# A two-layer perceiver block: the keys' constant, the norms' powers and the values' bias computed elsewhere, and a new order

## The chip, the cores and the metric

The kernel runs on one core of one Trainium2 chip. A core has TensorE (PE, matrix products into PSUM), VectorE (DVE), ScalarE (ACT), GpSimd (POOL) and SyncE (SP), which here starts all transfers. Each engine runs its own instructions in order; engines wait for each other on semaphores. The metric is the device time of one execution in microseconds (us), lower is better; a kernel's time is the median of its runs.

## The reference

The input `x` has 128 batches of 32 tokens, 256 wide; the context `ctx` has 128 batches of 257 rows, 256 wide. Six residual steps follow each other:

```
x = x + xattn0(ctx, layernorm(x))        # softmax attention of x over the 257 context rows
x = x + scan(layernorm(x))               # gated selective scan, 512 channels x 16 states, 32 steps
x = x + mlp0(layernorm(x))               # ternary weights, gelu, layernorm inside, hidden 1024
x = x + xattn1(layernorm(x), ctx, ctx)   # focused linear attention over the context, 16 heads
x = x + attn1(layernorm(x))              # attention among the 32 tokens, low-rank keys and values
x = x + mlp1(layernorm(x))               # quantized activations (127 steps), ternary weights
```

The change sits mostly in `xattn1`, cut here to what matters:

```
def feature(x, scale):
    x = (relu(x) + 1e-6) / scale
    xp = x ** 3
    return xp / norm(xp) * norm(x)
q = feature(input_q @ Wq + bq, sp)
k = feature(input_k @ Wk + bk, sp)
v = input_v @ Wv + bv
z = 1 / (einsum(q, k.sum(axis=2)) + 1e-6)
kv = einsum('bhjc,bhjd->bhcd', k, v)
out = einsum('bhic,bhcd->bhid', q, kv) * z
```

## The kernel before

**Tiling.** Four batches make a group: 4 x 32 = 128 tokens, one row of a tile each. There are 32 groups, taken in nine blocks of 2, 4, 4, 4, 4, 4, 4, 4 and 2 groups (`BLOCKS`). For each group, `context_group` loads its context, computes `xattn0` and then sums `k` times `v` over the 257 keys for `xattn1` (result `kvc`; the last context row is treated apart, through `pl`, `vl`, `plg`, `vlz`). For each block, `scan_block` does the scan for all its tokens at once (up to 512 columns). For each group, `latent_group` then runs `mlp`, `linear` (the query side of `xattn1`), `attention` and `quantized_mlp`, and stores the group.

**Order.** Nothing runs where it is written. Every call on `R` is recorded, with the engines that could do it (`R.either` is DVE or POOL; `relu`, `copy`, `cast`, `scaled` and `minus_column` also offer two), its duration as estimated by `ns_of`, and the operations it needs. `Recorder.order` then places all operations in a list schedule: each part of the work has a span of due times in `DUE`, an operation's due time lies inside its part's span, and of the operations that can start within `WINDOW` of the first, the one with the earliest wanted time is taken. Where an operation has several engines, `chosen` takes the one with the smallest sum of start and duration times (1 + `PRICE` of the engine). `trace` emits the result and chains the instructions of each engine in exactly that order; its line L575 issues every recorded instruction, which is why the trace shows that line nearly everywhere. Where the plan leaves TensorE idle for more than 600 ns, `keep_busy` (L562) adds matmuls of constants. Buffers come from rings of fixed size.

**Keys and values.** For two batches at a time, `keys` forms the keys `z` in PSUM (tile `pkey`): a matmul of ones with `bk3` brings in the scaled bias, three bf16 parts that add up to it, then come the products with `wkv[:, 0]`. `bk3` is built during setup from `bk` by way of `parts`: four row groups of 32 with the same content, of which batch i of the pair uses rows 32 i to 32 i + 2. `keys_values` then makes `u = relu(z)` (ACT, tile `ku`), adds the constant `e1` = 1e-6/scale on POOL, and calls `cubed`. That takes sums of squares on ACT (tile `ks`, with sums in `kn`), multiplies on POOL to get the cube, takes sums of squares again, raises the two sums to the powers 1/2 and -1/2 in one POOL operation with the tile `halves`, and multiplies the two into the factor `f` (tile `kf`). The values (`pval`) are scaled by `f` on ACT into `vf`, whose seventeenth column per head is `f` itself, and `pk` collects the sums over keys. For the queries, `cubed` runs once per group with the inverse factor (tiles `ls`, `ln`, `lf`).

**Norms.** `stats` takes mean and variance on DVE (`st`, `mv`) and `rstd_of` forms (variance + eps) to the power -1/2 in two POOL operations (`rstd`). `norm` then writes `xn = (x - mean) * rstd` on DVE. In `scan_block` this runs for each group, followed by the addition of `b_out` on POOL, transposes into `xTs`, the projections `pproj` and, per state, `a` (ACT), the scan `h` (DVE) and the weighted sum `acc` (DVE) or `some` (POOL).

**Bias of the values.** `linear` multiplies `bv1` by the denominators `den` on POOL (tile `y`), adds the numerators from PSUM (`pn`) on DVE and multiplies by `zf` on DVE.

**Quantizing.** `quantize` forms 127/max as a reciprocal and a multiplication on DVE (`qm`), multiplies and rounds in two operations: for the 256-wide input on DVE and then POOL, for the 1024-wide one on POOL (DVE in the last block).

Of the kernel before, what the change touches and what calls it, by code (L numbers as in the profile page):

```python
# [16 lines left out]
P = 128  # L17
# [249 lines left out]
class Recorder:  # L267
# [62 lines left out]
    def record(self, calls):  # L330
        ways = {}
        for engine, (name, args, kw) in calls.items():
            out = kw.get("out", args[0] if args else None)
            rest = list(args[1:] if "out" not in kw else args)
            rest += [v for k, v in kw.items() if k not in ("out", "accum_out")]
            ins = [a for a in rest if is_ap(a)]
            outs = [a for a in (out, kw.get("accum_out")) if is_ap(a)]
            full = dict(kw)
            if name == "tensor_scalar":
                full |= dict(zip(("scalar1", "scalar2"), args[2:4]))  # L340
            if name == "scalar_tensor_tensor":
                full |= dict(zip(("scalar",), args[2:3]))
            if name == "activation":
                full |= dict(zip(("func",), args[2:3]))
            if engine == "gpsimd" and name == "tensor_tensor":
                full |= dict(zip(("op",), args[3:4]))
            n = size_of(out)
            ns = ns_of(engine, name, full, out, ins, n)
            table = TABLES.get(full.get("func")) if name == "activation" else None
            tensors = [  # L350
                a for a in ins if (size_of(a) > 1 or name == "tensor_tensor") and not in_psum(a)
            ]
            locks = engine == "gpsimd" and len(ins) > 0
            if engine == "vector":
                two = name in ("tensor_tensor", "scalar_tensor_tensor", "tensor_tensor_scan")
                fast = name in ("tensor_scalar", "tensor_copy") and not in_psum(out)
                locks = len(tensors) > 1 if two else fast and len(tensors) > 0 and n > 64
            ways[engine] = [(name, args, kw)], ns, locks
        reads = [b for b in map(box_of, ins) if b]
        writes = [b for b in map(box_of, outs) if b]  # L360
        bufs = [a.buf for a in (*ins, *outs) if isinstance(a, View)]
        self.keep += bufs
        self.bufs_of.update((id(b), b) for b in bufs)
        if self.joined is not None:
            small = ins[0].shape[0] < P or size_of(ins[0]) < P
            self.joined.append((*ways["tensor"][:2], reads, writes, small))
            return
        landing = 0
        if "sync" in ways:
            size = size_of(out) * P * 4 if writes else 0  # L370
            landing = 2000 + size / 180.0
        self.add(ways, reads, writes, table, landing)
# [218 lines left out]
PRICE = {"tensor": 0.0, "vector": 28.013093, "scalar": 4.356996, "gpsimd": 3.720234, "sync": 0.0}  # L591
WINDOW = 13.821085
SOONER = 0.0675
AHEAD = 0.744939
HORIZON = 1.665209
# [3 lines left out]
def perceiver_kernel(ctx: ExitStack, tc: tile.TileContext, t: dict, out: bass.AP):  # L599
# [30 lines left out]
    nc.gpsimd.memset(halves[:, 1, :], 0.5)  # L630
    ones = cst.tile([P, P], F32, name="ones")
# [96 lines left out]
    bv1 = row("bv1", t["bv1"], D)  # L728
# [36 lines left out]
    def cubed(u, n, tag, inverse=False):  # L765

        sq = (t2k if n == 2 else t1k)([P, n, D], f"{tag}s")
        nrm = tiny(f"{tag}n", [P, 2, n])
        for j in range(n):
            R.scalar.activation(sq[:, j, :], u[:, j, :], AF.Square, accum_out=nrm[:, 0, j : j + 1])  # L770
        R.gpsimd.tensor_tensor(u, sq, u, ALU.mult)
        for j in range(n):
            R.scalar.activation(sq[:, j, :], u[:, j, :], AF.Square, accum_out=nrm[:, 1, j : j + 1])
        powers = halves[:, 0:2, 0:n] if inverse else halves[:, 1:3, 0:n]
        R.gpsimd.tensor_tensor(nrm, nrm, powers, ALU.pow)
        f = tiny(f"{tag}f", [P, n])
        R.gpsimd.tensor_tensor(f, nrm[:, 0, :], nrm[:, 1, :], ALU.mult)
        return f
# [58 lines left out]
    R.vector.tensor_tensor(bk, bk, col, ALU.mult)  # L837

    parts = t1k([P, 2, 4, 32], "bkp")
    R.gpsimd.memset(parts, 0.0)  # L840
    for k in range(3):
        part = ring("bkb", 1).tile([P, 2], "bkb", BF16)
        R.vector.tensor_copy(part, bk)
        R.vector.tensor_copy(parts[:, :, :, k], part.unsqueeze(2).to_broadcast([P, 2, 4]))
        if k < 2:
            R.vector.tensor_tensor(bk, bk, parts[:, :, 0, k], ALU.subtract)
# [24 lines left out]
    R.vector.tensor_scalar(p_l[:, 0, :], pkl[:, 0:D], 0.0, None, ALU.max)  # L871
    R.vector.tensor_tensor(p_l[:, 0, :], p_l[:, 0, :], e1, ALU.add)
# [88 lines left out]
    def stats(xg):  # L961

        st = tiny("st", [P, 6])
        R.vector.bn_stats(st, xg)
        mv = tiny("mv", [P, 2])
        R.vector.bn_aggr(mv, st)
        return mv, rstd_of(mv[:, 1:2], LN_EPS)

    def norm(xg):
        mv, r = stats(xg)  # L970
        xn = t1k([P, D], "xn")
        R.vector.tensor_scalar(xn, xg, mv[:, 0:1], r, ALU.subtract, ALU.mult)
        return xn, mv, r
# [19 lines left out]
    def context_group(b0, xg, kvc):  # L993
# [91 lines left out]
        with R.together():  # L1085
            for m in range(8):
# [6 lines left out]
                )  # L1093
        for b in range(0, GB, PAIR):
            zs = keys(cTs[b : b + PAIR])
            for i in range(PAIR):
                keys_values(cTs[b + i], zs[i], pk[:, :, b + i, :], b + i == GB - 1)
        v = pk.rearrange("p c b (h k) -> p h c b k", h=2)
        R.vector.tensor_scalar(kvc, v[:, 0], odd[:, 0:1], None, ALU.mult)
        R.vector.scalar_tensor_tensor(kvc, v[:, 1], odd[:, 1:2], kvc, ALU.mult, ALU.add)  # L1100

# [19 lines left out]
    def keys_values(cT, z, pk, last):  # L1121
        u = t2k([P, 2, D], "ku")
        R.relu(u, z)
        R.gpsimd.tensor_tensor(u, u, e1.unsqueeze(1).to_broadcast([P, 2, D]), ALU.add)
        f = cubed(u, 2, "k")
        R.first = (len(R.ops) - 3,)
# [10 lines left out]
        for j in range(2):  # L1137
            R.scalar.activation(
                vf[:, j, :, 0:16], pv[:, j * D : (j + 1) * D].rearrange("p (h k) -> p h k", k=16),
                AF.Copy, scale=f[:, j : j + 1],  # L1140
            )
        R.gpsimd.tensor_copy(vf[:, :, :, 16], f.unsqueeze(2).to_broadcast([P, 2, NH]))
        with R.together():
            for c in range(2):
                for j in range(2):
                    for m in range(4 * c, 4 * c + 4):
# [5 lines left out]
                        )  # L1152


    def scan_block(x, late):
# [3 lines left out]
        xT = ring("xTs", 1).tile([P, 2, TOK], "xTs")[:, :, 0:tok]  # L1159
        for g in range(size):  # L1160
            xn, _, _ = norm(x[g])
# [97 lines left out]
    def linear(xg, kvc):  # L1259
# [23 lines left out]
        with R.together():  # L1283
# [8 lines left out]
        den = tiny("den", [P, NH], 2)  # L1292
        R.vector.tensor_copy(den, pv[:, :, 16])
# [7 lines left out]
        R.gpsimd.tensor_tensor(  # L1301
            yv, bv1.rearrange("p (h k) -> p h k", k=16),
            den.unsqueeze(2).to_broadcast([P, NH, 16]), ALU.mult,
        )
        R.vector.tensor_tensor(yv, pv[:, :, 0:16], yv, ALU.add)
        R.vector.tensor_tensor(yv, yv, zf.unsqueeze(2).to_broadcast([P, NH, 16]), ALU.mult)
# [102 lines left out]
    def quantize(h, n, ms, k, amax, gamma, late):  # L1409
# [10 lines left out]
        R.vector.tensor_scalar(m, m, 127.0, None, ALU.mult)  # L1420
# [4 lines left out]
        engine = wide if n == HID else R.vector  # L1425
        engine.tensor_scalar(h, h, m, ROUND, ALU.mult, ALU.add)
        q = (t2k if n == HID else t1k)([P, n], f"q{n}", BF16)
        engine = wide if n == HID else R.gpsimd
# [84 lines left out]
    (-1.233024, -0.335498), (0.019828, 0.480193), (-1.629912, -0.869437), (-0.837897, -0.738361),  # L1513
    (-0.093681, -0.088914), (-0.021839, -0.017211), (0.306149, 0.488484), (0.39917, 0.543159),
    (0.505346, 1.339487), (0.48714, 0.600075), (0.577018, 0.904067), (0.865508, 1.005891),
    (1.046044, 1.425814), (1.390255, 1.643429), (1.317874, 1.43935), (1.798509, 1.951231),
    (2.102721, 2.277249), (2.253363, 2.602763), (2.83034, 2.835295), (1.877067, 1.881711),
    (1.451009, 1.899495), (0.786758, 1.881711), (1.887508, 2.002024), (0.636118, 0.718999),
    (0.728345, 0.76535), (0.753626, 0.774222), (0.721695, 1.041519), (1.02934, 1.176199),
    (1.193086, 1.242338), (1.482066, 1.506436), (1.570038, 1.574756), (1.52572, 1.568128),  # L1520
    (1.582666, 1.870871), (1.996577, 2.069774), (2.143081, 2.422113), (2.358304, 2.65149),
    (2.69793, 2.755759), (2.394754, 2.76594), (2.909432, 3.128141), (3.227729, 3.512565),
    (3.409932, 3.76627), (2.727973, 3.098836), (3.085723, 3.337484), (3.365331, 3.681179),
    (3.656735, 4.119898), (2.875393, 3.198347), (3.111345, 3.33781), (3.418247, 3.706203),
    (3.705912, 4.06225), (3.050509, 3.381501), (3.357332, 3.56083), (3.584301, 3.855628),
    (3.839172, 4.228837), (1.635373, 1.790687), (1.595887, 1.641535), (1.962785, 2.117782),
    (2.053357, 2.161526), (2.195383, 2.199528), (2.205476, 2.209605), (2.389908, 2.395792),
    (2.486901, 2.49243), (2.488439, 2.647508), (2.615044, 2.87897), (2.840922, 3.128108),
# [125 lines left out]
```

## Time and profile before

| what | value |
|---|---|
| three runs | 1712.74, 1715.9, 1718.06 us |
| median | 1715.9 us |
| first to last instruction of the profiled execution | 1714.2 us (its own device time is not given apart) |
| mean granted TensorE clock | 0.996 |
| idle time of DVE, ACT, POOL between instructions | 209.5, 286.8, 345.3 us |
| share of the 16 DMA engines, 0 to 100 us | 0.52 |
| the same, 1000 to 1100 us | 0.11 |

The busy time of an engine is the time covered by its instructions. The chain of waits follows the last instruction back to what released it, step by step; its shares tell which engine the end was waiting for. PE's busy time contains the tails of pipelined matmuls: matmuls 256 wide in fp32 start 216 ns apart in a row, while a single one is shown with some 385 ns. In groups by shape, "128x4 f32<-128x4 f32" is the output and input (partitions x elements) of one instruction.

### The profile page before, as it was taken

The page shows a single profiled execution, that of the slowest core. Times are in us where ns is not written, and L with a number is a line of the kernel's source. Part 1 is how long each engine was busy: PE and PEld are TensorE (multiplying, and loading weights), DVE is VectorE, ACT ScalarE, POOL GpSimd, SP SyncE. Part 2 cuts the span into 40 slices and gives each one's busy share as a digit, 9 for nine tenths or more (in the row PEclk, how much of TensorE's full clock was granted, in tenths as well). Part 3 has the DMA queues.
Part 4 walks back from the last instruction along what each step waited for, and adds up shares of the span by engine and source line. Part 5 has one row for each costly group of instructions (what it writes and reads, how often), then busy time and mean ns, then how long its engine had stood idle before and what let it go on. Part 6 is the DMA issues. An engine that isn't in the chain of part 4 may idle for free.

```text
span 1714.2 us, 45797 instructions
## 1 busy us (share of the span) xinstructions
PE 1650.3 (96%) x17587; PEld 1200.9 (70%) x17587; DVE 1501.8 (88%) x2960; ACT 1422.8 (83%) x3484; POOL 1362.6 (79%) x2152
## 2 busy tenths in 40 slices
PE   8999999999999999999999999999999989899986
PEld 6778777767677767766777777777777666666664
DVE  5389699988997997959998997979999899999777
ACT  4587789888988899779888998889998888788676
POOL 6668769768795888688878678886898699788887
PEclk9999999999999999999999999999999999999999
DMA  8312100110010102001100012010110000000000
GB/s 235 99 60 72 30 29 30 57 35 7 29 54 5 35 14 63 30 2 45 38 30 29 8 42 63 3 29 10 61 42 30 2 20 8 4 4 2 5 9 22
DMA packets 44762, 59.74 MB, mean 35 GB/s; under 512 B 8704, under 2 KB 27008, under 8 KB 44544
## 3 DMA queue, kind: packets, MB, share of 16 engines
q1 hardware_dynamic: 44544, 56.81, 10.7%
q8 instruction: 139, 2.28, 0.6%
q14 instruction: 79, 0.65, 0.1%
HBM read 52.32 MB, written 4.19 MB: 33 GB/s over the span
## 4 chain that ended last, share of the span: by engine, by line
PE 48%; DVE 24%; ACT 15%; POOL 10%; issue 3%; DMA 0%; DVEq 0%; POOLq 0%; ACTq 0%; SPq 0%
DVE h L575 10%; PE pkey L575 7%; PE pproj L575 7%; PE pval L575 6%; DVE acc L575 5%; PE pT L575 3%; PE pmlp L575 3%; PE pqa L575 3%; POOL ku L575 3%; ACT a L575 2%; PE pk L575 2%; ACT ks L575 2%; ACT L575 2%; PE pka L575 2%; PE pcT L575 2%
## 5 line engine op out<-in xcount | busy, mean ns | idle before, releaser
L575 DVE TENSOR_TENSOR_SCAN h<-a,pproj 128x512 f32<-128x512 f32 (+1 forms) x576 | 613.9, 1087 | 22.6 <-ACT a L575 12.5
L575 ACT ACTIVATE a<-dl,a_neg 128x496 f32<-128x496 f32 (+1 forms) x576 | 367.5, 664 | 57.7 <-DVE h L575 53.6
L575 DVE SCALAR_TENSOR_TENSOR acc<-h,w_st,acc 128x512 f32<-128x512 f32 (+1 forms) x436 | 299.9, 688 | 0.7
L575 PE MATMUL pval<-wkv,cT 128*128 128x256 f32 x1024 | 243.9, 384 | 0.1
L575 PE MATMUL pkey<-wkv,cT 128*128 128x256 f32 x1024 | 238.1, 386 | 0.0
L575 ACT ACTIVATE ks<-ku 128x256 f32<-128x256 f32 x512 | 209.1, 415 | 19.3 <-POOL ku L575 17.9
L575 PEld LDWEIGHTS pkey<-wkv,cT 128*128 128x128 f32 x1024 | 189.3, 190 | 39.0 <-issue 15.6
L575 PEld LDWEIGHTS pval<-wkv,cT 128*128 128x128 f32 x1024 | 188.0, 190 | 32.0 <-issue 4.5
L575 POOL TENSOR_TENSOR ku<-ku,e 128x512 f32<-128x512 f32 x128 | 162.8, 1280 | 31.3 <-ACT ku L575 30.0
L575 POOL TENSOR_TENSOR ku<-ks,ku 128x512 f32<-128x512 f32 x128 | 164.4, 1290 | 16.9 <-ACT ks L575 15.8
L575 POOL TENSOR_TENSOR kn<-kn,halves 128x4 f32<-128x4 f32 x128 | 134.3, 1052 | 23.5 <-ACT ks L575 21.9
L575 ACT ACTIVATE vf<-pval,kf 128x256 f32<-128x256 f32 x256 | 108.3, 475 | 31.1 <-PE pval L575 26.3
L575 POOL TENSOR_TENSOR rstd<-rstd,halves 128x1 f32<-128x1 f32 x224 | 126.1, 567 | 6.1
L575 PE MATMUL pproj<-xTs,w_in 128*128 128x512 f32 (+1 forms) x288 | 122.8, 554 | 2.2 <-DVE x L575 1.3
L575 ACT ACT_TABLE_LOAD x95 | 121.9, 1283 | 2.3 <-DVE hq L575 0.6
L575 POOL TENSOR_TENSOR some<-some,h 128x512 f32<-128x512 f32 (+1 forms) x104 | 115.2, 1107 | 3.5
L575 PE MATMUL pmlp<-w_pr,hT 128*128 128x256 f32 x512 | 117.3, 383 | 0.6 <-DVE x L575 0.6
L575 PEld LDWEIGHTS pmlp<-w_pr,hT 128*128 128x128 f32 x512 | 96.2, 191 | 14.7 <-DVE x L575 0.7
L575 POOL TENSOR_SCALAR h<-h,w_st 128x512 f32<-128x512 f32 (+1 forms) x104 | 65.3, 629 | 51.0 <-DVE h L575 32.7
L575 ACT ACTIVATION_READ_ACCUMULATOR ks<-ku 128x1 f32 x512 | 100.8, 197 | 0.0
L575 POOL TENSOR_SCALAR rstd<-mv 128x1 f32<-128x1 f32 x224 | 45.4, 203 | 67.5 <-DVE mv L575 43.3
L575 PE MATMUL ph<-w_fc,x 128*128 128x512 bf16 x384 | 91.5, 380 | 0.3 <-ACT vf L575 0.2
(289 smaller groups left out, 3867.0 us busy)
## 6 DMA issues: line engine op xcount, KB each, us to landing
cx<-in_ctx_dram SPq DMA_DIRECT2D x64, 512.0 KB
x<-in_x_dram SPq DMA_DIRECT2D x32, 128.0 KB
cr<-in_ctx_dram SPq DMA_DIRECT2D x128, 32.0 KB
out_dram<-x SPq DMA_DIRECT2D x32, 128.0 KB
vlz<-vl SPq DMA_DIRECT2D x128, 1.1 KB
w_in<-in_w_inT_dram SPq DMA_DIRECT2D x1, 1024.0 KB
raw_fc<-in_w_fcT_dram SPq DMA_DIRECT2D x2, 512.0 KB
raw_pr<-in_w_prT_dram SPq DMA_DIRECT2D x2, 512.0 KB
```

What stands on the lines that cost most here:

```text
L575: ins = getattr(engine, name)(*(traced(a) for a in args), **{k: traced(v) for k, v in kw.items()}).ins
```

## The change

1. `bk3` is built from two columns, `bk + e1` and `bk`. The first batch of each pair reads the rows with the first one, so `u = max(z, e1)` in one DVE operation gives relu + e1. The second batch keeps relu on ACT and the addition on POOL. The row of `ctx` treated apart uses the first form too.
2. `cubed` takes the reciprocal of one sum of squares on DVE, multiplies by the other and raises the product to 1/2 in a single power half as wide. In `scan_block` the norms of all groups of a block share one power; its moments come first for all groups, then the power, then each group's `xn`.
3. `linear` no longer adds the values' bias: `context_group` adds bias times the sums of the keys to `kvc`, with two operations per group (tile `vb`). `bv1` comes as a column layout `bvc`, in 16 transfers in place of one.
4. `xn`, the multiplication by 127 and both steps of the narrow quantizing may run on DVE or POOL; the scaling of the values by `f` may be one DVE or two ACT operations. `record` takes lists of calls for that. The last batch of a group adds to `pk` after the other three.
5. `DUE` (every number, as many as before), `PRICE`, `WINDOW`, `SOONER`, `AHEAD` and `HORIZON` have new values.

```diff
-PRICE = {"tensor": 0.0, "vector": 28.013093, "scalar": 4.356996, "gpsimd": 3.720234, "sync": 0.0}
-WINDOW = 13.821085
-SOONER = 0.0675
-AHEAD = 0.744939
-HORIZON = 1.665209
+PRICE = {"tensor": 0.0, "vector": 903.348472, "scalar": 4.458506, "gpsimd": 4.513973, "sync": 0.0}
+WINDOW = 13.478919
+SOONER = 0.068234
+AHEAD = 0.632901
+HORIZON = 1.528864
...
-    bv1 = row("bv1", t["bv1"], D)
+    bvc = wts.tile([P, 2, 16], F32, name="bvc")
+    for c in range(2):
+        for h in range(8):
+            h_ = slice((c * 8 + h) * 16, (c * 8 + h + 1) * 16)
+            R.sync.dma_start(bvc[h * 16 : (h + 1) * 16, c, :], t["bv1"][:, h_].to_broadcast([16, 16]))
...
-        powers = halves[:, 0:2, 0:n] if inverse else halves[:, 1:3, 0:n]
-        R.gpsimd.tensor_tensor(nrm, nrm, powers, ALU.pow)
         f = tiny(f"{tag}f", [P, n])
-        R.gpsimd.tensor_tensor(f, nrm[:, 0, :], nrm[:, 1, :], ALU.mult)
+        R.vector.reciprocal(f, nrm[:, 1 - inverse, :])
+        R.either.tensor_tensor(f, f, nrm[:, inverse, :], ALU.mult)
+        R.gpsimd.tensor_tensor(f, f, halves[:, 1, 0:n], ALU.pow)
         return f
...
+    bks = tiny("bks", [P, 2, 2], 1)
+    R.vector.scalar_tensor_tensor(bks[:, :, 0], col, FOCUS_EPS, bk, ALU.mult, ALU.add)
+    R.vector.tensor_copy(bks[:, :, 1], bk)
...
+    def normed(xg, mv, r):
+        xn = t1k([P, D], "xn")
+        R.either.tensor_scalar(xn, xg, mv[:, 0:1], r, ALU.subtract, ALU.mult)
+        return xn
...
+        vb = t1k([P, 2, GB, 16], "vb")
+        R.either.tensor_tensor(
+            vb, bvc.unsqueeze(2).to_broadcast([P, 2, GB, 16]),
+            kvc[:, :, :, 16:17].to_broadcast([P, 2, GB, 16]), ALU.mult,
+        )
+        R.either.tensor_tensor(kvc[:, :, :, 0:16], kvc[:, :, :, 0:16], vb, ALU.add)
...
-        R.relu(u, z)
-        R.gpsimd.tensor_tensor(u, u, e1.unsqueeze(1).to_broadcast([P, 2, D]), ALU.add)
+        e12 = e1.unsqueeze(1).to_broadcast([P, 2, D])
+        if shifted:
+            R.vector.tensor_tensor(u, z, e12, ALU.max)
+        else:
+            R.relu(u, z)
+            R.gpsimd.tensor_tensor(u, u, e12, ALU.add)
...
-        for j in range(2):
-            R.scalar.activation(
-                vf[:, j, :, 0:16], pv[:, j * D : (j + 1) * D].rearrange("p (h k) -> p h k", k=16),
-                AF.Copy, scale=f[:, j : j + 1],
-            )
+        pvs = pv.rearrange("p (j h k) -> p j h k", j=2, k=16)
+        R.record({
+            "scalar": [
+                ("activation", (vf[:, j, :, 0:16], pvs[:, j], AF.Copy), {"scale": f[:, j : j + 1]})
+                for j in range(2)
+            ],
+            "vector": ("tensor_tensor", (
+                vf[:, :, :, 0:16], pvs,
+                f.unsqueeze(2).unsqueeze(3).to_broadcast([P, 2, NH, 16]), ALU.mult,
+            ), {}),
+        })
...
+        last = len(sums) == GB - 1
+        R.first = tuple(sums) if last else ()
...
+        mvs = tiny("mvs", [P, NG, 2], 1)
+        rs = tiny("rs4", [P, NG], 1)[:, 0:size]
         for g in range(size):
-            xn, _, _ = norm(x[g])
+            moments(x[g], mvs[:, g])
+        R.gpsimd.tensor_scalar(rs, mvs[:, 0:size, 1], LN_EPS, 1.0, ALU.add, ALU.mult)
+        R.gpsimd.tensor_tensor(rs, rs, halves4[:, 0:size], ALU.pow)
+        for g in range(size):
+            xn = normed(x[g], mvs[:, g], rs[:, g : g + 1])
             R.gpsimd.tensor_tensor(x[g], x[g], b_out, ALU.add)
...
-        den = tiny("den", [P, NH], 2)
-        R.vector.tensor_copy(den, pv[:, :, 16])
...
-        R.gpsimd.tensor_tensor(
-            yv, bv1.rearrange("p (h k) -> p h k", k=16),
-            den.unsqueeze(2).to_broadcast([P, NH, 16]), ALU.mult,
+        R.vector.tensor_tensor(
+            yv, pv[:, :, 0:16], zf.unsqueeze(2).to_broadcast([P, NH, 16]), ALU.mult
         )
-        R.vector.tensor_tensor(yv, pv[:, :, 0:16], yv, ALU.add)
-        R.vector.tensor_tensor(yv, yv, zf.unsqueeze(2).to_broadcast([P, NH, 16]), ALU.mult)
         R.gpsimd.tensor_tensor(xg, xg, y, ALU.add)
...
-        R.vector.tensor_scalar(m, m, 127.0, None, ALU.mult)
+        R.either.tensor_scalar(m, m, 127.0, 1.0, ALU.mult, ALU.mult)
...
-        engine = wide if n == HID else R.vector
+        engine = wide if n == HID else R.either
         engine.tensor_scalar(h, h, m, ROUND, ALU.mult, ALU.add)
         q = (t2k if n == HID else t1k)([P, n], f"q{n}", BF16)
-        engine = wide if n == HID else R.gpsimd
+        engine = wide if n == HID else R.either
         engine.tensor_scalar(q, h, -ROUND, 1.0, ALU.add, ALU.mult)
```

## The prediction

> **What bounds it now.** I read the page first (busy shares, chain), then the groups by shape, the waits, the busy time by stretch, and last the chain over the final 35 us. The trace puts every recorded instruction on L575, so I go by tile names.
>
> ```profile
> span 1714.2 us, 45797 instructions
> PE 1650.3 (96%) x17587; PEld 1200.9 (70%) x17587; DVE 1501.8 (88%) x2960; ACT 1422.8 (83%) x3484; POOL 1362.6 (79%) x2152
> PE 48%; DVE 24%; ACT 15%; POOL 10%; issue 3%; DMA 0%; DVEq 0%; POOLq 0%; ACTq 0%; SPq 0%
> ```
>
> No engine alone sets the end: the chain changes hands, spending 48% of the span on PE, 24% on DVE, 15% on ACT, 10% on POOL. PE's 96% contains pipeline tails, so it is not proof that PE is full. The busy times by stretch (stretch; length, then busy us of PE, PEld, DVE, ACT, POOL) show two regimes:
>
> ```profile
> 900.00:1000.00 100.00, 99.00 (x1095) 69.79 (x1094) 90.89 (x169) 90.44 (x213) 79.18 (x121) 1.00 0.09 28
> ...
> 1400.00:1500.00 100.00, 90.61 (x710) 65.47 (x709) 96.18 (x160) 83.55 (x185) 86.98 (x132) 0.98 0.02 5
> 1500.00:1600.00 100.00, 90.67 (x973) 62.94 (x974) 90.73 (x237) 79.82 (x184) 86.68 (x148) 0.97 0.01 4
> 1600.00:1714.00 114.00, 94.62 (x1393) 66.80 (x1378) 86.14 (x246) 77.09 (x153) 92.02 (x162) 0.98 0.04 12
> ```
>
> In the middle PE has hardly a hole. After 1400 us the keys are done, PE is idle 314 - 275.9 = 38.1 us, and DVE and POOL carry the load.
>
> **Which engine gets the free choices.** The planner compares start + duration x (1 + price). With the new prices an xn costs POOL about 0.565 x 5.51 = 3.1 us, DVE 0.406 x 904 = 367 us. So every new "either" lands on POOL, unless POOL is over 360 us behind; and values scaled by f stay two ACT instructions (2 x 0.475 x 5.46 = 5.2 us against hundreds). That alternative therefore changes nothing.
>
> **Part by part.** Prices come from these groups (count | busy us, mean ns | idle before):
>
> ```profile
> L575 POOL TENSOR_TENSOR ku<-ku,e 128x512 f32<-128x512 f32 x128 | 162.8, 1280 | 31.3 <-ACT ku L575 30.0 <-DVE xn L575 0.5
> L575 POOL TENSOR_TENSOR kn<-kn,halves 128x4 f32<-128x4 f32 x128 | 134.3, 1052 | 23.5 <-ACT ks L575 21.9
> L575 POOL TENSOR_TENSOR rstd<-rstd,halves 128x1 f32<-128x1 f32 x224 | 126.1, 567 | 6.1
> L575 ACT ACTIVATE ku<-pkey 128x512 f32<-128x512 f32 x128 | 73.0, 592 | 11.8 <-PE pkey L575 9.7 <-PE pT L575 1.4 <-PE poa L575 0.3
> L575 DVE TENSOR_SCALAR xn<-x,mv,rstd 128x256 f32<-128x256 f32 x96 | 48.8, 522 | 20.6 <-POOL rstd L575 18.9 <-ACT ls L575 1.5
> L575 DVE TENSOR_SCALAR xn<-xn,qm 128x256 f32<-128x256 f32 x32 | 13.4, 420 | 0.2
> L575 POOL TENSOR_SCALAR h<-h,w_st 128x256 f32<-128x256 f32 x32 | 15.3, 482 | 12.5 <-DVE h L575 12.3
> L575 DVE TENSOR_TENSOR p<-pq,e 128x256 f32<-128x256 f32 x32 | 13.2, 413 | 0.1
> L575 DVE RECIPROCAL qm<-top 128x1 f32<-128x1 f32 x64 | 9.9, 156 | 0.6
> ```
>
> *POOL.* Half of the 128 additions of e1 go: -81.4. The keys' power shrinks from 128x4 to 128x2 (128x2 rows: 712 ns): 128 x 0.71 - 134.3 = -43.4; the queries' from 128x2 (23.3 us) to 128x1 (33 x 0.567): -4.6. The product of norms stays. The scan's 32 pairs rstd (0.203 + 0.563) become seven of 1.25 and two of 0.91: 10.6 - 24.5 = -13.9. The y<-bv,den product goes: -19.9. Together -163.2. Added: 96 xn. No row has a two-pointer 128x256 tensor_scalar; below it lies 482 (one pointer), above it 1118 (128x1024). A pointer costs 83 ns (dq, two pointers, 369, against rstd, none, 203, halved), so 565: +54.2. Quantizing's 32 multiplications at 482: +15.4; 64 times 127/x at 203: +13.0; vb's two 128x128 operations lie between 210 (128x2) and 623 (y, 128x256), linearly 415: 64 x 0.415 = +26.6. Together +109.2, **net -54.0**.
>
> *DVE.* The 64 maxima 128x512 from PSUM lie between 413 (half the width) and 742 (acc, same width): 413 plus the 267 that acc gains from 256 to 512 = 680, +43.5. Reciprocals 128x2 lie between 156 and 244 (128x16): 162 x 128 = 20.7, the queries' 33 x 0.156 = 5.1. Removed: xn 48.8, xn<-xn,qm 13.4, the 127s 9.2, den 5.2, y<-pn,y 13.1, and 3.3 from y x zf. **Net -23.7.** *ACT* loses 64 relus, 73.0 / 2: **-36.5**. PE's matmuls keep their number and shape.
>
> What of this is on the path? I weigh each engine's relief by chain share over busy share, as if the path met its instructions at random: POOL 54.0 x 10/79 = 6.8, DVE 23.7 x 24/88 = 6.5, ACT 36.5 x 15/83 = 6.6: **-19.9**. The bounds are 0 (other work was ending just as late) and -54 (POOL's whole relief).
>
> A rule of the skill speaks against moving xn. The Trainium skill, "Perfetto Trace Analysis", Optimizing Scalar/DVE Operations, warns that shifting work between DVE and GpSimd might not help since they share a read port. The trace agrees in part: on DVE xn takes 326 ns at best, 1506 at worst, 522 in the mean. If by that rule xn and its quantizing relieved DVE of nothing, 62.2 x 24/88 = 17 us of the gain would go.
>
> Moved work costs as follows. **Start:** bv1's single DMA becomes 16, 15 more issues on SP at about 22 us. SP rows there last 0.42 to 0.78 us, so 7 us at 0.47; wqa, woa, wupk, wupv, then x, cx, cr of the second group, the MLP weights and wkaT queue behind. PE and DVE wait for these; bounds 0 and +12, I take +3. **Tail:** here the chain sits on POOL:
>
> ```profile
> 1683.13 1.11 POOL hq L575
> 1684.24 0.33 POOL msq L575
> 1684.57 1.01 POOL q L575
> ...
> 1692.42 0.41 POOL q L575
> 1692.83 0.66 POOL dq L575 x2
> ```
>
> Between 1682 and 1693 us two xn, three xn<-xn,qm and three 127s now run on DVE beside it; on POOL they add 2 x 0.565 + 3 x 0.482 + 3 x 0.203 = +3.2. All six last groups would give 6 x (0.565 + 0.482 + 0.406) = +8.7, another order 0. **Block starts:** the scan's norms wait for the last group's moments, and POOL then does one power and four xn in a row: 1.255 + 4 x 0.565 = 3.52 us against 0.77 + 0.406 (xn's median on DVE) = 1.17. That is 2.35 x 7 + 0.88 x 2 = 18.2 us; with the 0.75 us b_out additions between the xn, 35.3. Behind them wait the transposes, pproj and DVE's scan, which already idles for the first ACT results. At the chain's DVE share of 24%: +4.4, bounds 0 and +35.3. **Waits:** the reciprocal puts ACT's sums of squares before DVE's queue, where the next scan stands:
>
> ```profile
> POOL kn L575 <- ACT ks L575: 21.9, 24, 3.7
> DVE xn L575 <- POOL rstd L575: 18.9, 9, 7.3
> ```
>
> The first wait moves from POOL to DVE at most whole (+21.9); the second leaves DVE (-18.9). I set these against each other. The new order itself has no row: it could close part of the tail's 38.1 us of PE idleness or open as much; I take 0.
>
> Sum: -19.9 + 3 + 3.2 + 4.4 = -9.3, against the profiled span of 1714.2: 1704.9. The page gives no time around the span; the median of the three runs is 1715.9 (1712.74 to 1718.06), 1.7 above, which I keep: **1706.6 us**.
>
> **Rivals.**
> A, the forecast: 1706.6, its own range 1695 to 1711; chance 0.44.
> B, released load plus a better tail: the costs of the moves hide and the search closes a third of the tail's PE holes, -19.9 - 12.7: 1683. For it: DVE and POOL, both relieved overall, bound that tail. Against it: POOL's relief lies before 1480, where the keys are; in the tail POOL gains work. Chance 0.16.
> C, PE is the bound in the middle after all: the relief only counts after 1400 us, 314/1714 of 19.9 = -3.6, plus 3 and 3.2: 1718.5. For it PE's 99 of 100 us there; against it 52% of the chain that is not PE. Chance 0.10.
> D, slower: the block starts. If two thirds of the 35.3 us are exposed, -13.7 + 23.5 = +9.8: 1725.7. For it: the last group's x is ready just before its xn, DVE already waits for ACT's `some` at block starts, 31.6 us in 14 waits. Against it: all groups but the last can be early, and DVE has latent-group work to fill in. It decides from 13.7 us exposed (39%), and shows from 18.8 (53%). Chance 0.30.
>
> **Numbers.** Under 0.3%, about 5 us, a measurement can't tell a change. A and B are faster, 0.60; C the same, 0.10; D slower, 0.30. The range 1680 to 1731 leaves out the lower part of B and the upper of D (up to 1737.5 at full exposure), some 0.15 together.
>
> **What would show it.** POOL near 1309 us busy, DVE 1478, ACT 1386; kn's power 128 times at 0.71; xn wholly on POOL near 565 ns; 64 DVE maxima near 680; reciprocals whose idle time before, ended by ACT ks, stays under the 18.9 us that xn's waits lose. D shows as longer DVE idleness before pproj, released by `some`, at the nine block starts, B as PE idle under 30 us after 1400. I am wrong if POOL's busy time doesn't fall by some 50 us, or if it does and the chain's DVE or ACT share grows instead.

## The result and the profile after

| | before | after |
|---|---|---|
| median | 1716.98 us (1712.74 to 1718.06, 4 runs) | 1763.55 us (1759.92 to 1765.43, 4 runs) |
| ratio | | 1.0273, 95% interval 1.0257 to 1.0289 |
| profiled execution, first to last instruction | 1714.2 us | 1760.7 us (device time 1762.5) |

The changed kernel is 46.6 us slower. The page of the changed kernel, span, busy times and the chain:

```profile
span 1760.7 us, 45814 instructions
PE 1651.7 (94%) x17479; PEld 1199.3 (68%) x17541; DVE 1478.4 (84%) x2930; ACT 1390.3 (79%) x3426; POOL 1360.9 (77%) x2255
...
PE 35%; POOL 29%; DVE 21%; ACT 8%; issue 6%; DMA 1%; SPq 0%; POOLq 0%; DVEq 0%; ACTq 0%
DVE h L585 9%; PE pkey L585 6%; DVE acc L585 5%; POOL xn L585 5%; PE pval L585 4%; PE pproj L585 4%; POOL ku L585 3%; POOL rstd L585 3%; PE pT L585 3%; POOL some L585 3%; PE pmlp L585 2%; POOL x L585 2%; POOL kf L585 2%; POOL rms L585 2%; PE pk L585 2%
```

DVE's 1478 us were forecast at 1478, ACT's 1390 at 1386. POOL was forecast at 1309 and stayed at 1361. Its share of the chain went from 10% to 29%, and a name is there that was not there before: `POOL xn`. The groups by shape of the changed kernel (count | busy us, mean ns | idle before) say why, and show the other parts at their prices:

```profile
L585 POOL TENSOR_SCALAR xn<-x,mv,rstd 128x256 f32<-128x256 f32 x64 | 79.2, 1237 | 2.3
L585 POOL TENSOR_SCALAR xn<-x,mvs,rs 128x256 f32<-128x256 f32 x32 | 39.4, 1235 | 0.1
L585 POOL TENSOR_SCALAR xn<-xn,qm 128x256 f32<-128x256 f32 x32 | 15.2, 474 | 3.0
L585 POOL TENSOR_TENSOR kf<-kf,halves 128x2 f32<-128x2 f32 x128 | 91.5, 716 | 4.9
L585 DVE TENSOR_TENSOR ku<-pkey,e 128x512 f32<-128x512 f32 x64 | 43.1, 673 | 4.3 <-PE pkey L585 4.1
L585 DVE RECIPROCAL kf<-kn 128x2 f32<-128x2 f32 x128 | 19.3, 152 | 28.2 <-ACT ks L585 27.4 <-POOL kf L585 0.5
```

An xn takes 1236 ns on POOL; I had reckoned 565. On 96 of them that is 96 x 0.671 = 64 us of POOL time that the plan doesn't know of either (the formula in `ns_of` gives 195 + 2 x 75 + 0.83 x 256 = 557 ns). The multiplication of the same tile by qm, the same shape, takes 474. What waits for xn is in the waits of the changed kernel (who waits <- for whom: total us, times, longest):

```profile
DVE amax L585 <- POOL xn L585: 30.3, 22, 4.6
PEld pT L585 <- POOL xn L585: 29.9, 37, 1.8
PE pT L585 <- POOL xn L585: 19.3, 30, 1.6
```

And the busy time by stretch (stretch; length, then busy us of PE, PEld, DVE, ACT, POOL) shows the tail, where POOL is nearly full and the others wait:

```profile
1600.00:1700.00 100.00, 85.04 (x1136) 59.73 (x1140) 62.74 (x175) 62.11 (x140) 91.18 (x157) 0.95 0.02 6
```

### The profile page after: what moved, and what is told of

It reads as the page before. It is cut to its first block, busy times and chain, and to the rows that moved or that the text cites. A ratio compares the mean times of both kernels' runs of the same rounds, so it can differ in the third digit from the quotient of the medians.

```text
span 1760.7 us, 45814 instructions
## 1 busy us (share of the span) xinstructions
PE 1651.7 (94%) x17479; PEld 1199.3 (68%) x17541; DVE 1478.4 (84%) x2930; ACT 1390.3 (79%) x3426; POOL 1360.9 (77%) x2255
## 4 chain that ended last, share of the span: by engine, by line
PE 35%; POOL 29%; DVE 21%; ACT 8%; issue 6%; DMA 1%; SPq 0%; POOLq 0%; DVEq 0%; ACTq 0%
DVE h L585 9%; PE pkey L585 6%; DVE acc L585 5%; POOL xn L585 5%; PE pval L585 4%; PE pproj L585 4%; POOL ku L585 3%; POOL rstd L585 3%; PE pT L585 3%; POOL some L585 3%; PE pmlp L585 2%; POOL x L585 2%; POOL kf L585 2%; POOL rms L585 2%; PE pk L585 2%
## 5 line engine op out<-in xcount | busy, mean ns | idle before, releaser
L585 POOL TENSOR_TENSOR ku<-ku,e 128x512 f32<-128x512 f32 x64 | 82.3, 1285 | 68.4 <-ACT ku L585 66.4
L585 POOL TENSOR_TENSOR rstd<-rstd,halves 128x1 f32<-128x1 f32 x192 | 106.8, 559 | 6.8
L585 POOL TENSOR_TENSOR kf<-kf,halves 128x2 f32<-128x2 f32 x128 | 91.5, 716 | 4.9
L585 POOL TENSOR_SCALAR rstd<-mv 128x1 f32<-128x1 f32 x192 | 38.6, 201 | 65.9 <-DVE mv L585 45.1
```

Of the source, the lines that this page charges most:

```text
L585: ins = getattr(engine, name)(*(traced(a) for a in args), **{k: traced(v) for k, v in kw.items()}).ins
```

## The experiments

Each run is set beside the kernel before on the same chip, whose median was 1716.7 to 1718.0 in all of them.

**First: parts of the change, planned anew.** Four kernels, all planned by the list schedule from the changed due times.

`e1_xn_dve`, all xn on DVE:

```diff
-        R.either.tensor_scalar(xn, xg, mv[:, 0:1], r, ALU.subtract, ALU.mult)
+        R.vector.tensor_scalar(xn, xg, mv[:, 0:1], r, ALU.subtract, ALU.mult)
```

> The changed kernel with all 96 xn = (x - mean) * rstd on DVE again; nothing else differs, the order is planned anew from the same due times. Theory S (one slow instruction: xn took 1237 ns on POOL where I had reckoned 565, 65 us of POOL time that the plan does not know of): POOL busy falls by about 119 us to some 1242, xn on DVE near 520 ns, time 1700 to 1715. Rival W (DVE's new waits on ACT's sums, kf behind ks 27 us): POOL falls as much, the time only to 1740 to 1755. Rival O (the new due times and prices are bad by themselves): 1745 or more.

Measured 1796.99 us, ratio 1.046 (1.0444 to 1.0475): 33 us slower than the changed kernel, although POOL's busy time fell to 1248.7 us. S and W missed; the time lies in the open range of O, which the second group of runs has to answer.

`e2_xn_priced`, in `ns_of`:

```diff
             pointers = sum(is_ap(kw.get(k)) for k in ("scalar1", "scalar2"))
+            if pointers == 2 and n == D:
+                return 1240
             return 195 + 75 * pointers + 0.83 * n
```

> The changed kernel with xn still on POOL, but the plan is told that it lasts 1240 ns. The load on every engine is that of the changed kernel, only the order knows of it. If the harm is that everything behind xn comes later than planned: 1715 to 1735. If it is the 65 us of POOL time and the latency of xn themselves, planned or not: 1745 to 1765. Rival W: unchanged, 1755 to 1765.

Measured 1785.41 us, ratio 1.0393 (1.0377 to 1.0408), above all three ranges. All 96 xn are still on POOL (1228 and 1220 ns). A plan that knows the true duration is worse than one that doesn't.

`e3_xn_multadd`:

```diff
-        R.either.tensor_scalar(xn, xg, mv[:, 0:1], r, ALU.subtract, ALU.mult)
+        nb = tiny("nb", [P, 1])
+        R.gpsimd.tensor_scalar(nb, mv[:, 0:1], r, -1.0, ALU.mult, ALU.mult)
+        R.either.tensor_scalar(xn, xg, r, nb, ALU.mult, ALU.add)
```

> The changed kernel with xn on POOL as x * rstd + nb, nb = -mean * rstd from one more POOL operation of one column; both scalars are still read per partition. If the subtraction is what makes the instruction slow: xn near 565 ns, POOL busy about 64 - 33 = 31 us lower, time 1725 to 1745. If two per-partition scalars over 256 columns are slow whatever the operation: xn stays near 1237 ns and the time rises to 1765 to 1790.

Measured 1780.98 us, ratio 1.0369 (1.0352 to 1.0386). The time lies in the second range, that of a slow form that stays, but the instruction itself took the short time of the first (groups by shape of this run):

```profile
L585 POOL TENSOR_SCALAR xn<-x,rstd,nb 128x256 f32<-128x256 f32 x64 | 35.2, 550 | 1.7
L585 POOL TENSOR_SCALAR nb<-mv,rstd 128x1 f32<-128x1 f32 x64 | 17.2, 269 | 5.5
```

With two per-partition scalars, the same tile and the same engine, 550 ns: it is the subtraction.

`e4_order_alone`, the kernel before with the changed `DUE`, `PRICE`, `WINDOW`, `SOONER`, `AHEAD` and `HORIZON`:

> The kernel before with the changed kernel's due times, prices and windows, none of its other edits. Theory S: the order alone does little, 1705 to 1735, no engine's busy time moves by more than 5 us. Rival O: 1745 to 1765.

Measured 1822.34 us, ratio 1.0601 (1.0585 to 1.0617), above both ranges and 104 us slower than the same operations under their own due times. The four runs lie 63 to 104 us above the kernel before, so due times do not carry over to other durations or operations. Changing one duration and planning anew changes the whole order, and such a run can't tell what the one duration was worth. From here on the order is held.

**Second: the same order, one instruction different.**

`f1_same_order_xn_dve` (in `trace`, after the plan is made; `is_xn`, not shown, picks the 96 instructions):

```diff
+            if is_xn(op):
+                op.ways = {"vector": op.ways[op.engine]}
+                op.engine = "vector"
             engine = getattr(self.nc, op.engine)
```

> The changed kernel in exactly the order that its own plan gives, only that each of the 96 xn is issued to DVE at its place in that order instead of to POOL. After the first runs due times can no longer be moved to other durations without harm, so the order is held. Theory S (the 65 us by which xn on POOL lasts longer than planned are the loss): 1705 to 1730, although DVE gets some 50 us more. Rival W (waits of DVE for ACT's sums) and rival D (block starts): 1745 or more, since both stay.

Measured 1725.01 us, ratio 1.0059 (1.0037 to 1.0082), inside the range of S and far under that of W and D. The operations are those of `e1_xn_dve`, on the same engines but for three casts; that run has some 134 more filling matmuls of constants besides, which its plan asks for. This one is 72 us faster, by the order.

`f2_add_for_subtract`:

```diff
-        R.either.tensor_scalar(xn, xg, mv[:, 0:1], r, ALU.subtract, ALU.mult)
+        R.either.tensor_scalar(xn, xg, mv[:, 0:1], r, ALU.add, ALU.mult)
```

> The changed kernel in exactly its own order, xn on POOL, but the mean is added where it was subtracted (the output is another); no other instruction differs. Theory S: xn takes 550 to 570 ns as in the multiply-add run, 96 x 0.68 = 65 us of POOL time vanish, and the rest of my prediction is tested: 1700 to 1715. Rivals W and D: 1740 or more.

Measured 1716.99 us over 10 runs, ratio 1.0000 (0.9988 to 1.0012). That is 2 us above the range of S; W and D are out. Nothing but the arithmetic operation of 96 instructions differs from the changed kernel, and its whole loss is gone. With it rival O is gone: the new due times are no loss under the operations that they came with. The page and the groups by shape of this run:

```profile
PE 1639.3 (96%) x17479; PEld 1196.6 (70%) x17541; DVE 1476.9 (86%) x2930; ACT 1385.5 (81%) x3426; POOL 1296.8 (76%) x2255
...
PE 47%; DVE 23%; POOL 17%; ACT 8%; issue 4%; POOLq 0%; DVEq 0%; ACTq 0%
```

```profile
L585 POOL TENSOR_SCALAR xn<-x,mv,rstd 128x256 f32<-128x256 f32 x64 | 36.4, 569 | 2.3
L585 POOL TENSOR_SCALAR xn<-x,mvs,rs 128x256 f32<-128x256 f32 x32 | 17.6, 557 | 0.1
```

xn lies at the reckoned 565, and POOL's share of the chain falls from 29% to 17%. But the loads are now those of my forecast (DVE 1477, ACT 1386, POOL 1297), and the time is not 1706.6 but that of the kernel before.

`f3_before_same_order_xn_pool` does the reverse to the kernel before: its order, xn issued to POOL with the subtraction.

> The kernel before in its own order, only the 96 xn issued to POOL at their places, with the subtraction: 119 us more POOL time, 49 us less DVE time, nothing of it planned. Theory S: 1755 to 1790. If POOL's slack covers it: 1717 to 1735.

Measured 1763.06 us, ratio 1.0276 (1.0258 to 1.0294). That single edit costs the old kernel 45 us, about what the whole change cost.

`f4_before_same_order_xn_pool_add`, the same with the addition:

> As the run before this one, with the mean added in place of subtracted (the output is another): 53 us more POOL time in place of 119. The difference of the two runs is what the slow instruction itself costs in another order: theory S says 25 us or more, and this run at 1722 to 1745. If the two agree within 8 us, the length of xn is not what costs.

Measured 1721.09 us over 10 runs, ratio 1.0026 (1.0014 to 1.0038), a little under the expected range. The groups by shape of the two runs:

```profile
L583 POOL TENSOR_SCALAR xn<-x,mv,rstd 128x256 f32<-128x256 f32 x96 | 121.0, 1263 | 1.5 <-PE pka L583 0.2
L583 POOL TENSOR_SCALAR xn<-x,mv,rstd 128x256 f32<-128x256 f32 x96 | 57.8, 605 | 1.5 <-PE pka L583 0.2
```

The slow form is worth 42.0 us here, 46.6 us in the changed order; moving xn to POOL at 605 ns each costs 3 to 4 us. The cost does not go with POOL's load: the move with the addition puts 49 us more on POOL (1362.6 to 1411.2) and takes 37 from DVE for these 3 to 4 us, while the next 64 us on POOL (to 1475.2) cost 42. Whether those 42 come from POOL being taken or from each xn arriving later, these runs don't separate.

**Third: which forms are slow.** `e5_forms_on_pool` puts 28 instructions ahead of the kernel before, where nothing else is in their way:

```diff
+    for _, args in (
+        ("fsubmul", (a_, b_, ALU.subtract, ALU.mult)),
+        ("fsub", (a_, 1.0, ALU.subtract, ALU.mult)),
+        ("fsubimm", (1.0, 1.0, ALU.subtract, ALU.mult)),
+        ("fmulsub", (a_, b_, ALU.mult, ALU.subtract)),
+        ("faddmul", (a_, b_, ALU.add, ALU.mult)),
+        ("fmuladd", (a_, b_, ALU.mult, ALU.add)),
+        ("fmaxmul", (a_, b_, ALU.max, ALU.mult)),
+    ):
+        for _ in range(4):
+            nc.gpsimd.tensor_scalar(fx, fx, *args)
```

> The kernel before with 28 operations put ahead of it on POOL, seven forms of tensor_scalar on one 128x256 tile, four of each: (x - p) * q, (x - p) * 1, (x - 1) * 1, x * p - q, (x + p) * q, x * p + q, max(x, p) * q, with p and q per-partition scalars. If subtraction itself is slow: the first four near 1200 ns, the others near 550. If only a subtraction of a per-partition scalar is: the third is near 400.

The groups by shape, one stretch after the other (one line for each of the seven forms, in the order of the code):

```profile
L777 POOL TENSOR_SCALAR a<-a,fp 128x256 f32<-128x256 f32 x4 | 4.9, 1221 | 0.2
L777 POOL TENSOR_SCALAR a<-a,fp 128x256 f32<-128x256 f32 x4 | 4.6, 1141 | 0.4
L777 POOL TENSOR_SCALAR a<-a 128x256 f32<-128x256 f32 x4 | 4.3, 1077 | 0.3
L777 POOL TENSOR_SCALAR a<-a,fp 128x256 f32<-128x256 f32 x4 | 4.9, 1218 | 0.4
L777 POOL TENSOR_SCALAR a<-a,fp 128x256 f32<-128x256 f32 x4 | 2.2, 554 | 0.4
L777 POOL TENSOR_SCALAR a<-a,fp 128x256 f32<-128x256 f32 x4 | 2.2, 554 | 0.4
L777 POOL TENSOR_SCALAR a<-a,fp 128x256 f32<-128x256 f32 x4 | 4.9, 1217 | 0.4
```

The third line is the subtraction of an immediate (a constant in the instruction): slow too. Slow is every form tried with a subtraction, in the first place or in the second, with a scalar per partition or without; and the maximum, which I had expected at 550, is just as slow. Addition and multiplication take 554 in either order. The run itself took 1742.66 us, a single run with the 28 instructions in its start.

**Fourth: why the lighter load gave nothing.**

`c1_negative_mean` is the changed kernel in its own order with all of its computation: beside each norm's power, ACT makes -mean (73 operations of some 0.2 us), and xn is (x + (-mean)) * rstd on POOL.

> The changed kernel in its own order, with the right output: 73 small ACT operations beside each norm's power make -mean, and xn on POOL is (x + (-mean)) * rstd. Theory S: xn at 550 to 570 ns and 1713 to 1726, 37 us or more under the changed kernel; ACT gets some 15 to 20 us of work that it has room for.

Measured 1717.20 us over 12 runs, ratio 1.0002 (0.9992 to 1.0013), inside the expected range; xn takes 570 ns.

`c2_tail_on_dve` is that kernel and moves, in the same order, to DVE what the plan has on POOL after 1300 us (`TAIL_FROM`) of xn, of the narrow quantizing's multiplication and of the multiplication by 127, 74 instructions in all:

```diff
+            moved = (
+                op.engine == "gpsimd" and op.at > TAIL_FROM and name == "tensor_scalar"
+                and (args[-2:] == (ALU.subtract, ALU.mult)
+                     or args[0].buf.name == "xn" or args[0].buf.name == "qm")
+            )
+            if moved:
+                op.ways = {"vector": op.ways["gpsimd"]}
+                op.engine = "vector"
```

> As the run before this one, and after 1300 us of the plan xn (with the subtraction), the narrow quantizing's multiplication and the multiplication by 127 go to DVE in the same order. If POOL in the tail is where the gain of the middle was given back: 4 to 10 us under the run before. If the tail hangs on the chain of dependent steps whichever engine does them: within 3 us of it.

Measured 1716.46 us, ratio 0.9996 (0.9988 to 1.0004): 0.7 us under `c1_negative_mean`, no difference that the runs can tell. POOL in the tail is not where the gain went.

`g1_no_reciprocal` is `f2_add_for_subtract` without the keys' 128 reciprocals:

> The run with the mean added (1717), in the same order, without the 128 reciprocals of the keys' factor: POOL multiplies the two sums of squares as they are (the factor is another number). What is left open is why engine loads that fell as reckoned (POOL 1297, DVE 1477, ACT 1386) gave no time. If DVE's new in-order waits for ACT's sums take the 9 us that I forecast: 1700 to 1709. If they are covered: 1712 to 1717.

Measured 1713.57 us, ratio 0.9986 (0.9977 to 0.9994): 3.4 us by the medians and 2.4 by the ratios for the reciprocals and their waits together, inside the range for waits that are covered.

`h1_before_less_pool`, `h2_before_less_dve` and `h3_before_less_both` ask the plain question, on the kernel before in its own order, by skipping instructions. The first one's edit in `trace` is:

```diff
+            if name == "tensor_tensor" and args[-1] == ALU.add and name_of(args[0]) == "ku":
+                adds += 1
+                if adds % 2:
+                    continue
```

> The kernel before in its own order, without every second addition of e1 to the keys (64 of 128, the output lacks 1e-6/scale there): 81 us less on POOL, nothing added anywhere. If relief is worth its share of the chain as I reckoned (81 x 10/79): 10 us, 1707. If the path hardly feels POOL: 1713 to 1717.

> The kernel before in its own order, without 64 multiplications by 127, 32 multiplications of the narrow quantizing and 32 additions of y on DVE (the output is another): 36 us less on DVE. By the chain share (36 x 24/88): 10 us, 1707. If the path hardly feels it: 1713 to 1717.

> Both omissions together: 81 us less on POOL and 36 us less on DVE. By chain shares -20 us, 1697. If relief of these engines is not felt while the order stands and PE carries the middle: 1710 to 1716, and then my term of -19.9 was wrong in kind and not in the waits that the change adds.

Measured 1713.82, 1713.80 and 1712.72 us; ratios 0.9980 (0.9971 to 0.9989), 0.9981 (0.9971 to 0.9991) and 0.9975 (0.9964 to 0.9986). All three lie in the range for a path that hardly feels the relief. The old kernel's own runs spread from 1712.7 to 1718.6 us beside them, so gains of 3 to 5 us are small, though the intervals leave out 1. DVE's busy time fell by 25 us only, POOL's by the expected 80. The page of the run with both, busy times and chain:

```profile
PE 1651.5 (97%) x17587; PEld 1205.6 (70%) x17587; DVE 1476.9 (86%) x2832; ACT 1419.1 (83%) x3484; POOL 1282.1 (75%) x2088
...
PE 62%; DVE 16%; ACT 13%; POOL 6%; issue 3%; DVEq 0%; ACTq 0%; POOLq 0%
```

The chain gave up 8 points of DVE, 4 of POOL and 2 of ACT, and PE took 14. The path hardly became shorter; it went another way of almost the same length.

`h4_before_less_pe` skips two of six matmuls in each accumulation into `ph`:

> The kernel before in its own order, without two of the six matmuls of each accumulation into ph (128 of 384; the output changes slightly or more): 128 x 0.216 = 28 us less PE work, with nothing taken from DVE, ACT or POOL. If PE carries the time: 12 to 25 us, 1693 to 1706. If the path answers to PE as little as to the others (about 6% of what is taken): 1713 to 1717.

Measured 1712.03 us, ratio 0.9979 (0.9971 to 0.9988): 4.7 us by the medians, a little under the range of a small answer, for 128 matmuls; PE's busy time fell from 1650.3 to 1627.7 us. PE is no single bound either.

## Why the prediction was wrong

**The term that failed** is "a pointer costs 83 ns ..., so 565: +54.2". The xn cost 96 x 1.236 = 118.6 us. My bounds were 482 and 1118, both from rows that multiply or add; no tensor_scalar of the old trace subtracts or takes a maximum on POOL, so no row showed the price, and the number of pointers, on which I reckoned, was the wrong property. `f2_add_for_subtract` and `f3_before_same_order_xn_pool` show that this one form is the whole loss. The prediction's own sign of being wrong came with it: POOL's busy time did not fall. The Trainium skill, "GPSIMD Engine Reference", When to use GPSIMD, calls operations with one tensor input roughly line-rate on GpSimd and prefers VectorE for elementwise work. These runs agree with the preference (522 ns on DVE before, 1236 on POOL after); the same one-input form at 554 and at 1218 ns shows that the first part depends on the operation.

**The weight** failed too. The right price alone does not give the time: by the prediction's own weight the missing 64.4 us on POOL are 64.4 x 10/79 = 8.2 us, and 1706.6 would have become some 1715. They cost 46.6.

**The relief of 19.9 us** was wrong in kind. Without the slow form the loads fell as reckoned or more, and the time did not. On the old kernel, the run with less POOL and less DVE work gives 4.8 us where chain shares would give 80 x 10/79 + 25 x 24/88 = 17. A share of the chain says where the path went, not what the path would be without it: that run's chain, now 62% on PE, found another way of almost the same length. In its order 80 us off POOL give 3.7 us, 25 us off DVE 3.7, 23 us off PE 4.7. To add is another matter: the 64 us more on POOL than planned cost 46.6. The doubt whether moved work relieves DVE at all can be laid down: its busy time fell by 23.4 us, against 23.7 reckoned.

**The losses.** *Waits:* I set the reciprocals' against xn's; the reciprocals with their waits are worth 2.4 to 3.4 us. *Start:* the +3 for 16 transfers did not show. The first of DVE's pproj operations starts at 79.9 us in the changed kernel and at 95.8 in the old one, under another order; the transfers were not tried alone. *Tail:* moving that work back brings 0.7 us, within the noise, so +3.2 was probably too much. *Block starts:* DVE's waits for `some` fell, though rival D said that they would grow; the batched norms were not undone alone. The lines, before and after:

```profile
DVE pproj L575 <- ACT some L575: 31.6, 14, 8.9
DVE pproj L585 <- ACT some L585: 22.7, 14, 9.1
```

**The rivals.** D had the right side by the wrong mechanism. C, "the relief only counts after 1400 us", comes close in time to what the change is without the slow form (1717.0 against 1718.5), but by luck: its reason, PE as the bound, does not fit the last run, in which less PE work gave as little as less of the others. B is wrong.

**The engine choice** held: every free choice went to POOL, the values stayed on ACT. It was not the plan's short duration that sent the 96 xn there: in `e2_xn_priced` the plan reckons with 1240 ns and they stay, since DVE's price of 903 outweighs it. I asked only what the load would be; the question to ask was what this very instruction costs on the engine to which the price sends it.

What stays open: which of the remaining parts cancel the small relief, and whether the slow form costs by POOL's time or by xn's delay. The runs of the change without its slow form that leave nothing out lie at the kernel before: 1717.20 and 1716.46 us. No version here beats the old kernel with all of its computation.

## What to carry to other kernels

Before an operation is moved to another engine, find a row with the same arithmetic operation there, not only the same shape: the formula that knows shape and pointers alone gave 557 ns for what took 1236. Under a held order, removing work was worth little here (3 to 5 us for 23 to 105), and the price of added work depended on how much was added: 49 us on POOL, with 37 off DVE, cost 3 to 4, the next 64 cost 42. So neither is to be read off a chain share. And to test a part of such a change, hold the order and exchange the instruction: planned anew, nearly the same instructions on the same engines differed by 72 us.

## What the runs showed of the hardware

On POOL, tensor_scalar on 128x256 fp32 takes 554 ns with additions and multiplications by per-partition scalars, and 1141 to 1221 ns when one of its two operations is a subtraction (in either place) or the first is a maximum; with immediates alone a subtraction takes 1077 (`e5_forms_on_pool`). In the kernel, replacing the subtraction by the addition of a negated mean brings xn from 1236 to 570 ns (`c1_negative_mean`). A subtraction by tensor_tensor is not affected in this way: xc, which reads the mean as a broadcast column, takes 613 ns and one of two full tiles (xT) 672; an addition of the same shape takes 727 (lines of the changed kernel):

```profile
L585 POOL TENSOR_TENSOR xc<-x,mv 128x256 f32<-128x256 f32 x32 | 19.6, 613 | 1.2
L585 POOL TENSOR_TENSOR xT<-xT,x 128x256 f32<-128x256 f32 x32 | 21.4, 672 | 2.9 <-ACT x L585 2.3
L585 POOL TENSOR_TENSOR x<-x,b 128x256 f32<-128x256 f32 x32 | 23.3, 727 | 0.5
```

On DVE, in the kernel before, the same xn with its subtraction has a median of 406 ns and a mean of 522.
